# Layer 3's expert feed-forward: an expert's rows turned between the two products of the expert before it, and result rows scattered to their tokens' rows in DRAM

## Chip, cores and metric

The kernel runs on one core of one Trainium2 chip. The metric is the device time of one execution in microseconds (us), given as the median of three runs.

## The reference

The whole model has four layers on 2 images of 256 channels and 48 x 48 pixels, so T = 4608 tokens of C = 256 numbers. The change touches the second half of layer 3 alone, a mixture of eight experts in which each token goes to one expert:

```
x = layer-normalised tokens, [4608, 256]
idx  = argmax(softmax(x @ gate_w + gate_b))      # the token's expert
prb  = that expert's probability
pos  = the token's place among the tokens of its expert, in token order
kept = pos < 720                                 # capacity: ceil(1.25 * 4608 / 8)
buf[idx, pos] = x                                # 8 x 720 slots of 256; others stay zero
hmid = relu(buf @ w1[e] + b1[e])                 # 256 -> 1024
ybuf = hmid @ w2[e] + b2[e]                      # 1024 -> 256
y    = ybuf[idx, min(pos, 719)] * prb * kept     # dropped tokens get zero
t    = t + nan_to_num(y, 0, 1e4, -1e4)
```

With the reference's own inputs (seed 0) the router is very uneven. Counting `idx` in the reference gives 0, 0, 0, 3148, 37, 804, 607 and 12 tokens for experts 0 to 7. With the capacity of 720 that leaves 2096 slots of 5760 with a token, 3664 empty slots (all of experts 0, 1 and 2, nearly all of 4 and 7), and 2512 tokens that are dropped.

## The kernel before

Activations are kept with channels on the partitions: `E.xres` is the residual stream, [128, 2, 4608], in SBUF for the whole kernel. Layers 0 to 2 and layer 3's attention come first. While that attention runs, class `Gate` works behind it: `take` writes the normalised tokens as rows of 256 numbers to DRAM (`xt_d`), and `place` works out for each slot which token it holds. It leaves three small tables in SBUF: `token` (the token of each slot; an empty slot gets token 0), `share_s` (its probability; zero for an empty slot) and `get` (for each token the row of `ybuf` with its result; the zero row behind the last slot for a dropped token). A slot is known by its expert, one of six groups (`JT`) and one of 120 places in the group (`JP`).

`layer3` then has two stages, each in pools of its own, and all instructions stand in program order on in-order engines, but for what the framework's scheduler moves.

**Experts**, for e in 0 to 7. The weights of e + 1 are asked for on SP's queue (L1742 to L1746). GpSimd issues six indirect gathers of 120 rows of 1 KB from `xt_d` into `xe` (L1770). TensorE turns them with twelve 120x120 transposes into `tp` (L1779, two PSUM buffers), VectorE copies four `tp` into `xT` (L1783). The first product `ph` (L1790) has 64 matmul instructions, since an f32 matmul is two; ScalarE writes `hid` with relu (L1794). The second product `py` (L1805) has 96 instructions over six groups. Two groups at a time VectorE adds the bias (L1809), multiplies by the share (L1811), and builds `fin`, the value with NaN and infinities replaced (L1817 to L1823); `fin` has two buffers and is first set to zero by GpSimd (L1815). SP stores `fin` to its slots' rows in `ybuf` (L1825).

**Return**, for 36 blocks of 128 tokens. GpSimd gathers each token's row of `ybuf` by `get` (L1835, six buffers), TensorE turns it with two transposes (L1841), VectorE adds it to `xres` (L1843). `store_out` (L1850) then has SP store `xres` to the output in twelve pieces of 384 KB, each as soon as its three blocks are done.

Of the kernel before, what the change touches and what calls it, by code (L numbers as in the profile page):

```python
# [1451 lines left out]
class Gate:  # L1452
# [8 lines left out]
    def __init__(self, E, keep, wp):  # L1461
        nc, p = E.nc, E.p
        self.JP = JP = self.CAP // self.JT
        self.NJ = NJ = self.NX * self.JT
        NX = self.NX
        self.wp = wp
        self.xt_d = E.dram.tile([T, C], F32, name="xt_d")
        self.get = keep.tile([P, NT], I32, name="get")
        self.token = keep.tile([JP, NJ], I32, name="token")
        self.share_s = keep.tile([JP, NJ], F32, name="share_s")  # L1470

        self.tg = wp.tile([P, 2, P + NX], F32, name="tg")
        nc.sync.dma_start(self.tg[:, :, P:], p["m_gate_w"].rearrange("(k p) e -> p k e", p=P))
        nc.vector.tensor_copy(self.tg[:, :, :P], bc(E.ident, [P, 2, P], 1))
        self.lg = wp.tile([P, NT, NX], F32, name="lg")

        self.gsum = wp.tile([P, NX], F32, name="gsum")
        self.both = wp.tile([P, NX], F32, name="both")
        self.gb = wp.tile([P, NX], F32, name="gb")
        nc.sync.dma_start(self.gb, p["m_gate_b"].partition_broadcast(P))  # L1480
        ids_i = wp.tile([P, P], I32, name="ids_i")
        nc.gpsimd.iota(ids_i, pattern=[[1, P]], base=0, channel_multiplier=0)
        self.ids = wp.tile([P, P], F32, name="ids")
        nc.vector.tensor_copy(self.ids, ids_i)
        part_i = wp.tile([P, 1], I32, name="part_i")
        nc.gpsimd.iota(part_i, pattern=[[0, 1]], base=0, channel_multiplier=1)
        part = wp.tile([P, 1], F32, name="part")
        nc.vector.tensor_copy(part, part_i)
        self.upto = wp.tile([P, P], F32, name="upto")
        nc.vector.tensor_scalar(self.upto, self.ids, part, None, ALU.is_ge)  # L1490
        self.ones = wp.tile([P, P], F32, name="ones")
        nc.vector.memset(self.ones, 1.0)

        tid_i = wp.tile([P, NT], I32, name="tid_i")
        nc.gpsimd.iota(tid_i, pattern=[[P, NT]], base=1, channel_multiplier=1)
        self.tid = wp.tile([P, NT], F32, name="tid")
        nc.vector.tensor_copy(self.tid, tid_i)

        self.before = wp.tile([P, NX], F32, name="before")
        nc.vector.memset(self.before, 0.0)  # L1500
        self.table = wp.tile([JP, 2, NJ], F32, name="table")
# [48 lines left out]
    def place(self, E, a, b, ps):  # L1550
# [90 lines left out]
            nc.vector.tensor_scalar(self.token, self.table[:, 0, :], -1.0, 0.0, ALU.add, ALU.max)  # L1641
            nc.vector.tensor_copy(self.share_s, self.table[:, 1, :])

        nc.vector.scalar_tensor_tensor(pos, idx, float(CAP), pos, ALU.mult, ALU.add)
        nc.vector.tensor_tensor(pos, pos, over, ALU.add)
        nc.vector.tensor_scalar(self.get[:, bs], pos, float(NX * CAP), None, ALU.min)
        yield


# [71 lines left out]
def layer3(ctx, E):  # L1721

    nc, tc, p = E.nc, E.tc, E.p
    NX, FT, CAP, JT = Gate.NX, 8, Gate.CAP, Gate.JT
    JP = CAP // JT
# [1 line left out]
    FMAX = 3.4028234663852886e38  # L1729
    keep = ctx.enter_context(tc.tile_pool(name="l3keep", bufs=1))  # L1730
    wts = ctx.enter_context(tc.tile_pool(name="l3wt", bufs=2))
    ybuf = E.dram.tile([NX * CAP + 1, C], F32, name="ybuf")
    limit = keep.tile([P, 2, C], F32, name="limit")
    nc.vector.memset(limit[:, 0, :], 1e4)
    nc.vector.memset(limit[:, 1, :], -1e4)
    zero = keep.tile([1, C], F32, name="zero")
    nc.vector.memset(zero, 0.0)
    nc.sync.dma_start(ybuf[NX * CAP : NX * CAP + 1, :], zero)

    def weights(e):  # L1740
        w1 = wts.tile([P, 2, FT * P], F32, tag="w1", name="w1")
# [8 lines left out]
    with (  # L1750
# [3 lines left out]
        gate = Gate(E, keep, gp)  # L1754
        layer3_attn(E, gate, psl)
        run(gate.place(E, NT - gate.TG, NT, psl))
    token, share_s, get = gate.token, gate.share_s, gate.get

    with (
        tc.tile_pool(name="l3x", bufs=2) as wp,  # L1760
        tc.tile_pool(name="l3xps", bufs=2, space=PSUM) as ps,
    ):
        for e in range(NX):
            w1, w2, b2 = ready
            if e + 1 < NX:
                ready = weights(e + 1)
            xe = wp.tile([JP, JT, C], F32, tag="xe", name="xe")
            for j in range(JT):
                o = e * JT + j
                nc.gpsimd.indirect_dma_start(  # L1770
                    out=xe[:, j, :], out_offset=None, in_=gate.xt_d[:, :],
                    in_offset=bass.IndirectOffsetOnAxis(ap=token[:, o : o + 1], axis=0),
                )
            xT = wp.tile([P, 2, CAP], F32, tag="xT", name="xT")
            for k in range(2):
                for g in range(2):
                    tp = ps.tile([P, HC], F32, tag="tp", name="tp")
                    for j in range(JT // 2):
                        nc.tensor.transpose(  # L1779
                            tp[:, j * JP : (j + 1) * JP],  # L1780
                            xe[:, g * (JT // 2) + j, k * P : (k + 1) * P], E.ident[:JP, :JP],
                        )
                    nc.vector.tensor_copy(xT[:, k, g * HC : (g + 1) * HC], tp)  # L1783
            hid = wp.tile([P, FT, CAP], F32, tag="hid", name="hid")
            for f in range(FT):
                for g in range(2):
                    gs = slice(g * HC, (g + 1) * HC)
                    ph = ps.tile([P, HC], F32, tag="ph", name="ph")
                    for k in range(2):
                        nc.tensor.matmul(  # L1790
                            ph, lhsT=w1[:, k, f * P : (f + 1) * P], rhs=xT[:, k, gs],
                            start=k == 0, stop=k == 1,
                        )
                    nc.scalar.activation(  # L1794
                        hid[:, f, gs], ph, AF.Relu, bias=E.v("m_b1", e * FT + f, 1)
                    )

            JG = 2
            for j0 in range(0, JT, JG):
# [19 lines left out]
                for s, op in enumerate((ALU.is_gt, ALU.is_lt)):  # L1819
                    inf = wp.tile([JP, JG, C], I32, tag="inf", name="inf")  # L1820
                    nc.vector.tensor_scalar(inf, ye, -FMAX if s else FMAX, None, op)  # L1821
                    for j in range(JG):
                        nc.vector.copy_predicated(fin[:, j, :], inf[:, j, :], limit[:JP, s, :])  # L1823
                o = e * CAP + j0 * JP
                nc.sync.dma_start(  # L1825
                    ybuf[o : o + JG * JP, :].rearrange("(j p) d -> p j d", p=JP), fin
                )

    with (
        tc.tile_pool(name="l3y", bufs=6) as wp,  # L1830
        tc.tile_pool(name="l3yps", bufs=4, space=PSUM) as ps,
    ):
        for i in range(NT):
            yt = wp.tile([P, C], F32, tag="yt", name="yt")
            nc.gpsimd.indirect_dma_start(  # L1835
                out=yt, out_offset=None, in_=ybuf[:, :],
                in_offset=bass.IndirectOffsetOnAxis(ap=get[:, i : i + 1], axis=0),
            )
            yp = ps.tile([P, 2, P], F32, tag="yp", name="yp")
            for k in range(2):  # L1840
                nc.tensor.transpose(yp[:, k, :], yt[:, k * P : (k + 1) * P], E.ident)  # L1841
            xr = E.xres[:, :, i * P : (i + 1) * P]
            nc.vector.tensor_tensor(xr, xr, yp, ALU.add)  # L1843


def store_out(E):
# [98 lines left out]
```

## Time and profile before

| | us |
|---|---|
| median of 3 runs | 5459.55 (5452.36 to 5462.36) |
| profiled execution, own time | 5504.47 |
| profiled execution, span of its trace | 5502.7 |
| layer 3's experts, first gather to last `fin` | 5064.2 to 5439.9 |
| return and output, first `yt` gather to the end | 5443.2 to 5502.7 |

The profile is one execution, some 0.8% longer than the median. "PE" is TensorE, "DVE" VectorE, "ACT" ScalarE, "POOL" GpSimd, "SPq" the sync engine's DMA queue. Times are us from the span's start. In the timeline a row holds start, duration, engine, line, operation, out<-in with shapes, the number of instructions, and in square brackets the idle time ahead of them with what ended it. In the table by windows a row holds the window, its length, the busy time of PE, PE's weight loads, DVE, ACT and POOL with their counts, the granted TensorE clock, the busy share of the 16 DMA engines and the GB/s that they moved.

### The profile page before, as it was taken

How to read it: one execution, taken by the hardware profiler on the slowest of the kernel's cores; microseconds unless marked ns; L12 is line 12 of the kernel's file. 1: busy time of each engine (PE TensorE's matmuls, PEld its weight loads, DVE VectorE, ACT ScalarE, POOL GpSimd, SP SyncE). 2: the span in 40 equal slices, each digit the busy share in tenths (PEclk: the TensorE clock that was granted, in tenths of full speed). 3: DMA queues.
4: the chain of work that ended last, by engine and by line, in shares of the span. 5: the costliest groups of instructions: out<-in, count | busy, mean ns of one | idle time of the engine just before them, and what ended most of it. 6: DMA issues, size and time to landing. Idle time of an engine off the chain costs nothing. (4 is left out here: it accounts for less than half of the span.)

```text
span 5502.7 us, 47222 instructions
## 1 busy us (share of the span) xinstructions
PE 4797.7 (87%) x15246; PEld 2649.9 (48%) x15246; DVE 3499.6 (64%) x5380; ACT 2371.5 (43%) x4935; POOL 2398.4 (44%) x1295
## 2 busy tenths in 40 slices
PE   7888788888877787879999999998799999998996
PEld 3444344444333343435555555565455555554664
DVE  4899988888999888999994234456534401212333
ACT  5767777666767566622222123322023322222220
POOL 3888887888989888830000000048412100001112
PEclk8999999999999899999999899999899999999997
DMA  4444444443444444421100100111111100001323
GB/s 155 166 171 177 165 178 160 160 157 137 173 150 173 150 161 153 151 100 37 41 26 2 39 1 0 37 38 24 14 58 46 46 6 6 9 6 23 83 76 80
DMA packets 173646, 486.56 MB, mean 88 GB/s; under 512 B 31487, under 2 KB 96516, under 8 KB 173124
## 3 DMA queue, kind: packets, MB, share of 16 engines
q1 hardware_dynamic: 165252, 471.82, 24.3%
q0 software_dynamic: 8128, 11.55, 1.6%
q8 instruction: 124, 2.03, 0.1%
q14 instruction: 142, 1.16, 0.1%
HBM read 416.44 MB, written 66.86 MB: 88 GB/s over the span
## 5 line engine op out<-in xcount | busy, mean ns | idle before, releaser
L344 PE MATMUL yp<-hc,ident 128*128 128x384 f32 x3072 | 1199.9, 523 | 293.7 <-DVE hc L390 253.8
L359 POOL TENSOR_TENSOR db<-dtu,bb 128x1536 f32<-128x1536 f32 x384 | 1333.3, 3473 | 45.5 <-issue 16.5
L344 PEld LDWEIGHTS yp<-hc,ident 128*128 128x128 f32 x3072 | 574.7, 198 | 875.3 <-DVE hc L390 451.3
L390 POOL TENSOR_TENSOR hc<-ho,cc 128x384 f32<-128x384 f32 x576 | 582.6, 1020 | 183.6 <-DVE ho L382 81.9
L390 DVE TENSOR_TENSOR hc<-hs,cc 128x384 f32<-128x384 f32 x960 | 501.3, 544 | 38.9 <-PE yp L344 37.7
L376 ACT ACTIVATE hs<-dt,negab 128x384 f32<-128x384 f32 x768 | 435.2, 582 | 92.6 <-DVE ho L385 41.4
L376 ACT ACTIVATE hs<-dt,negaf 128x384 f32<-128x384 f32 x768 | 434.6, 582 | 58.4 <-DVE hc L390 27.7
L385 DVE TENSOR_TENSOR_SCAN hs<-hs,state,db 128x384 f32<-128x384 f32 x400 | 396.6, 1015 | 55.8 <-POOL db L359 30.3
L382 DVE TENSOR_TENSOR_SCAN hs<-hs,state,db 128x384 f32<-128x384 f32 x400 | 397.1, 1014 | 30.0 <-POOL db L359 23.2
L1770 POOL DMA_INDIRECT xe<-xt_d,token x48 | 52.4, 1091 | 726.4 <-issue 715.0
L266 PE MATMUL mm<-xw,w_cv 128*128 128x384 f32 x768 | 288.8, 512 | 64.5 <-ACT xs L270 26.6
L1704 PE MATMUL po<-at,xtok 128*128 128x384 f32 x864 | 329.7, 506 | 7.7 <-ACT at L1702 7.5
L912 POOL PARTITION_ALL_REDUCE most<-most x1 | 0.4, 382 | 738.8 <-DVE most L911 738.8
L1354 PE MATMUL ph<-xn,w 128*128 128x384 f32 x768 | 292.9, 523 | 28.0 <-issue 10.4
L1695 PE MATMUL sp<-qT,xn 128*128 128x384 f32 x864 | 317.2, 486 | 0.0
L1702 ACT ACTIVATE at<-sp 128x384 f32<-128x384 f32 x216 | 104.9, 491 | 472.5 <-PE sp L1695 472.4
L1358 ACT ACTIVATE hid<-ph,vec 128x384 f32<-128x384 f32 x192 | 110.8, 582 | 338.8 <-PE ph L1354 254.5
L627 PE MATMUL pf<-t,wfc 128*128 128x384 f32 x768 | 255.4, 489 | 0.0
L646 PE MATMUL po<-hid,wfc 128*128 128x384 f32 x768 | 253.6, 486 | 0.0
L385 DVE TENSOR_TENSOR_SCAN ho<-hs,state,db 128x384 f32<-128x384 f32 x240 | 241.2, 1005 | 15.3 <-ACT hs L376 15.1
L382 DVE TENSOR_TENSOR_SCAN ho<-hs,state,db 128x384 f32<-128x384 f32 x240 | 240.3, 1001 | 6.3 <-ACT hs L376 6.2
L266 PEld LDWEIGHTS mm<-xw,w_cv 128*128 128x128 f32 x768 | 146.0, 196 | 192.7 <-ACT xs L270 43.2
(434 smaller groups left out, 7962.9 us busy)
## 6 DMA issues: line engine op xcount, KB each, us to landing
bb<-bcd SPq DMA_DIRECT2D x192, 768.0 KB
cc<-bcd SPq DMA_DIRECT2D x192, 768.0 KB
xw<-xi_d SPq DMA_DIRECT2D x24, 774.0 KB
w<-in_m_w SPq DMA_DIRECT2D x16, 1024.0 KB
y_d<-y SPq DMA_DIRECT2D x32, 384.0 KB
ye<-y_d SPq DMA_DIRECT2D x32, 384.0 KB
xi_d<-xz SPq DMA_DIRECT2D x48, 192.0 KB
z_d<-xz SPq DMA_DIRECT2D x48, 192.0 KB
```

Of the source, the lines that this page charges most:

```text
L266: nc.tensor.matmul(px, lhsT=w_cv[b, s][:, d * 4 + k, :], rhs=xw[:, d, o : o + W], start=k == 0, stop=k == 3,)
L344: nc.tensor.matmul(yp[d], lhsT=E.ident, rhs=hc, start=False, stop=summed[d] == NS)
L359: nc.gpsimd.tensor_tensor(db, bc(dtu[:, d, :], [P, GN, W], 1), bb, ALU.mult)
L376: nc.scalar.activation(hs, dt[:, d, :], AF.Exp, scale=nega[s][:, d * NS + n : d * NS + n + 1])
L382: nc.vector.tensor_tensor_scan(to, hs, db[:, j], init, ALU.mult, ALU.add)
L385: nc.vector.tensor_tensor_scan(to[:, ::-1], hs[:, ::-1], db[:, j, ::-1], init, ALU.mult, ALU.add)
L390: (nc.gpsimd if on_pool else nc.vector).tensor_tensor(hc, to, cc[:, j, :], ALU.mult)
L627: nc.tensor.matmul(pf, lhsT=wfc1[:, k, f * P : (f + 1) * P], rhs=t1[:, k, :], start=k == 0, stop=k == 1,)
L646: nc.tensor.matmul(po[m], lhsT=wfc2[:, f, m * P : (m + 1) * P], rhs=hid[:, i, :], start=f == 0, stop=f == 15,)
L1354: nc.tensor.matmul(ph, lhsT=w1[:, e, k, f * P : (f + 1) * P], rhs=xn[:, k, c * W : (c + 1) * W], start=k == 0, stop=k == 1,)
L1695: nc.tensor.matmul(sp, lhsT=xn[:, k, t0 + i * P : t0 + (i + 1) * P], rhs=qT[:, k, c * W : (c + 1) * W], start=k == 0, stop=k == 1,)
L1704: nc.tensor.matmul(po[m], lhsT=xtok[:, i, m * P : (m + 1) * P], rhs=at, start=i == 0, stop=i == MT - 1,)
```

## The change

Five things are edited together.

- `Gate.place` leaves out `get`. In its place it works out `out_row`: for each slot the token's row, and row T (4608) for an empty slot.
- `ybuf` is replaced by `y_tok`, [T + 1, 256] in DRAM, whose first T rows are set to zero by 36 stores of 128 KB on SP's queue. In the built program they stand on SP's queue right after layer 2's last small loads (L1265), with that layer's stores `y_d` and loads `ye` among and behind them.
- The gathers (`fetch`) and transposes (`turn`) become functions. Expert 0 is turned ahead of the loop, the rows of e + 1 are turned after the first product of e, and those of e + 2 are fetched after that. In the built program TensorE has, behind the last `ph` of an expert, six transposes, one `py` matmul, three transposes, one `py` matmul, three transposes, and the remaining `py`.
- Each `fin` is scattered by two indirect DMAs of 120 rows on GpSimd's queue to `y_tok` by `out_row`, where SP stored it to `ybuf` before. In the built program every scatter waits for the landing of the scatter before it, since both write `y_tok`; and the `memset` of a `fin` buffer stands right behind a pair of scatters and waits for the second.
- The return has twelve pieces of 384 tokens: one plain load on SP's queue (four buffers), six transposes, two adds. In the built program all twelve loads stand ahead of the twelve output stores on SP's queue; load n + 4 waits for the transposes of piece n.

```diff
@@ -1465,7 +1465,7 @@
         NX = self.NX
         self.wp = wp
         self.xt_d = E.dram.tile([T, C], F32, name="xt_d")
-        self.get = keep.tile([P, NT], I32, name="get")
+        self.out_row = keep.tile([JP, NJ], I32, name="out_row")
         self.token = keep.tile([JP, NJ], I32, name="token")
         self.share_s = keep.tile([JP, NJ], F32, name="share_s")
@@ -1641,9 +1641,11 @@
             nc.vector.tensor_scalar(self.token, self.table[:, 0, :], -1.0, 0.0, ALU.add, ALU.max)
             nc.vector.tensor_copy(self.share_s, self.table[:, 1, :])
-        nc.vector.scalar_tensor_tensor(pos, idx, float(CAP), pos, ALU.mult, ALU.add)
-        nc.vector.tensor_tensor(pos, pos, over, ALU.add)
-        nc.vector.tensor_scalar(self.get[:, bs], pos, float(NX * CAP), None, ALU.min)
+            none = self.wp.tile([JP, NJ], F32, tag="none", name="none")
+            nc.vector.tensor_scalar(none, self.table[:, 0, :], 0.0, float(T + 1), ALU.is_equal, ALU.mult)
+            nc.vector.scalar_tensor_tensor(
+                self.out_row, self.table[:, 0, :], -1.0, none, ALU.add, ALU.add
+            )
         yield
@@ -1729,13 +1732,14 @@
     FMAX = 3.4028234663852886e38
     keep = ctx.enter_context(tc.tile_pool(name="l3keep", bufs=1))
     wts = ctx.enter_context(tc.tile_pool(name="l3wt", bufs=2))
-    ybuf = E.dram.tile([NX * CAP + 1, C], F32, name="ybuf")
+    y_tok = E.dram.tile([T + 1, C], F32, name="y_tok")
     limit = keep.tile([P, 2, C], F32, name="limit")
     nc.vector.memset(limit[:, 0, :], 1e4)
     nc.vector.memset(limit[:, 1, :], -1e4)
-    zero = keep.tile([1, C], F32, name="zero")
-    nc.vector.memset(zero, 0.0)
-    nc.sync.dma_start(ybuf[NX * CAP : NX * CAP + 1, :], zero)
+    zero = keep.tile([P, C], F32, name="zero")
+    nc.gpsimd.memset(zero, 0.0)
+    for i in range(NT):
+        nc.sync.dma_start(y_tok[i * P : (i + 1) * P, :], zero)
     def weights(e):
         w1 = wts.tile([P, 2, FT * P], F32, tag="w1", name="w1")
@@ -1754,16 +1758,13 @@
         gate = Gate(E, keep, gp)
         layer3_attn(E, gate, psl)
         run(gate.place(E, NT - gate.TG, NT, psl))
-    token, share_s, get = gate.token, gate.share_s, gate.get
+    token, share_s, out_row = gate.token, gate.share_s, gate.out_row
     with (
         tc.tile_pool(name="l3x", bufs=2) as wp,
         tc.tile_pool(name="l3xps", bufs=2, space=PSUM) as ps,
     ):
-        for e in range(NX):
-            w1, w2, b2 = ready
-            if e + 1 < NX:
-                ready = weights(e + 1)
+        def fetch(e):
             xe = wp.tile([JP, JT, C], F32, tag="xe", name="xe")
             for j in range(JT):
                 o = e * JT + j
@@ -1771,9 +1772,12 @@
                     out=xe[:, j, :], out_offset=None, in_=gate.xt_d[:, :],
                     in_offset=bass.IndirectOffsetOnAxis(ap=token[:, o : o + 1], axis=0),
                 )
+            return xe
+        def turn(xe):
             xT = wp.tile([P, 2, CAP], F32, tag="xT", name="xT")
-            for k in range(2):
-                for g in range(2):
+            for g in range(2):
+                for k in range(2):
                     tp = ps.tile([P, HC], F32, tag="tp", name="tp")
                     for j in range(JT // 2):
                         nc.tensor.transpose(
@@ -1781,6 +1785,14 @@
                             xe[:, g * (JT // 2) + j, k * P : (k + 1) * P], E.ident[:JP, :JP],
                         )
                     nc.vector.tensor_copy(xT[:, k, g * HC : (g + 1) * HC], tp)
+            return xT
+        xT = turn(fetch(0))
+        xe = fetch(1)
+        for e in range(NX):
+            w1, w2, b2 = ready
+            if e + 1 < NX:
+                ready = weights(e + 1)
             hid = wp.tile([P, FT, CAP], F32, tag="hid", name="hid")
             for f in range(FT):
                 for g in range(2):
@@ -1794,6 +1806,10 @@
                     nc.scalar.activation(
                         hid[:, f, gs], ph, AF.Relu, bias=E.v("m_b1", e * FT + f, 1)
                     )
+            if e + 1 < NX:
+                xT = turn(xe)
+            if e + 2 < NX:
+                xe = fetch(e + 2)
             JG = 2
             for j0 in range(0, JT, JG):
@@ -1821,26 +1837,31 @@
                     nc.vector.tensor_scalar(inf, ye, -FMAX if s else FMAX, None, op)
                     for j in range(JG):
                         nc.vector.copy_predicated(fin[:, j, :], inf[:, j, :], limit[:JP, s, :])
-                o = e * CAP + j0 * JP
-                nc.sync.dma_start(
-                    ybuf[o : o + JG * JP, :].rearrange("(j p) d -> p j d", p=JP), fin
-                )
-
+                for j in range(JG):
+                    o = e * JT + j0 + j
+                    nc.gpsimd.indirect_dma_start(
+                        out=y_tok[:, :], in_=fin[:, j, :], in_offset=None,
+                        out_offset=bass.IndirectOffsetOnAxis(ap=out_row[:, o : o + 1], axis=0),
+                    )
+    TG = gate.TG
     with (
-        tc.tile_pool(name="l3y", bufs=6) as wp,
-        tc.tile_pool(name="l3yps", bufs=4, space=PSUM) as ps,
+        tc.tile_pool(name="l3y", bufs=4) as wp,
+        tc.tile_pool(name="l3yps", bufs=3, space=PSUM) as ps,
     ):
-        for i in range(NT):
-            yt = wp.tile([P, C], F32, tag="yt", name="yt")
-            nc.gpsimd.indirect_dma_start(
-                out=yt, out_offset=None, in_=ybuf[:, :],
-                in_offset=bass.IndirectOffsetOnAxis(ap=get[:, i : i + 1], axis=0),
+        for c in range(NT // TG):
+            yt = wp.tile([P, TG, C], F32, tag="yt", name="yt")
+            nc.sync.dma_start(
+                yt, y_tok[c * W : (c + 1) * W, :].rearrange("(i p) d -> p i d", p=P)
             )
-            yp = ps.tile([P, 2, P], F32, tag="yp", name="yp")
             for k in range(2):
-                nc.tensor.transpose(yp[:, k, :], yt[:, k * P : (k + 1) * P], E.ident)
-            xr = E.xres[:, :, i * P : (i + 1) * P]
-            nc.vector.tensor_tensor(xr, xr, yp, ALU.add)
+                yp = ps.tile([P, W], F32, tag="yp", name="yp")
+                for i in range(TG):
+                    nc.tensor.transpose(
+                        yp[:, i * P : (i + 1) * P], yt[:, i, k * P : (k + 1) * P], E.ident
+                    )
+                xr = E.xres[:, k, c * W : (c + 1) * W]
+                nc.vector.tensor_tensor(xr, xr, yp, ALU.add)
 def store_out(E):
```

## The prediction

> **What bounds the kernel now.** I read the cores first: one core, 5502.7 us, clock 0.949. The page then has TensorE busy for 87% of the span, but only layer 3's end is touched, from the first `xe` gather at 5064.2 to the end at 5502.7, so I read that stretch by its waits, timeline and windows. The waits between 5097 and 5440 us, seven of the eight experts:
>
> ```profile
> engine line waited for: us in total, times, longest us
> POOL fin L1815 <- DMA ybuf<-fin: 275.9, 17, 31.4
> PE ph L1790 <- DVE xT L1783: 16.1, 7, 2.3
> PE tp L1779 <- DVE xT L1783: 3.0, 7, 0.4
> ```
>
> TensorE sets the pace of the experts, and what stops it is one thing: at each change of expert it waits for `xT`, 16.1 + 3.0 = 19.1 us in 7 changes. GpSimd's long waits hold up nothing. The timeline of the last change and of the end:
>
> ```profile
> 5392.65 1.45 DVE L1823 COPY_PREDICATED fin<-inf,limit 120x256 f32<-120x256 int32 x4
> 5393.99 0.97 DVE L1783 COPY xT<-tp 128x360 f32<-128x360 f32 x2
> ...
> 5394.57 20.36 PE L1790 MATMUL ph<-xT,w 128*128 128x360 f32 x60 [2.30 <-DVE xT L1783]
> ...
> 5414.77 20.88 PE L1805 MATMUL py<-w,hid 128*120 128x256 f32 x96
> ...
> 5424.62 1.45 DVE L1823 COPY_PREDICATED fin<-inf,limit 120x256 f32<-120x256 int32 x4
> ...
> 5431.53 1.44 DVE L1823 COPY_PREDICATED fin<-inf,limit 120x256 f32<-120x256 int32 x4
> ...
> 5438.42 1.45 DVE L1823 COPY_PREDICATED fin<-inf,limit 120x256 f32<-120x256 int32 x4
> 5443.20 0.99 POOL L1835 DMA_INDIRECT yt<-ybuf,get  x1 [14.04 <-DMA ybuf<-fin]
> ...
> 5449.63 49.48 SPq L1850 DMA_DIRECT2D out<-xres  x12
> ```
>
> The two `xT` copies stand on VectorE behind the preceding expert's last `fin`; that is the wait. From the last expert's `py` (call its start S = 5414.77) the three `fin` end at S+11.3, S+18.2 and S+25.1, the return starts at S+28.4, and the end is at S+87.9: 59.5 us for return and output. Windows show what these are limited by:
>
> ```profile
> 5079.00:5093.00 14.00, 12.68 (x42) 7.71 (x41) 0.00 (x0) 5.51 (x10) 6.89 (x7) 1.00 0.87 79
> 5121.00:5123.00 2.00, 0.75 (x4) 0.17 (x2) 2.00 (x6) 0.00 (x0) 1.29 (x1) 1.00 1.00 345
> 5125.00:5131.00 6.00, 6.00 (x21) 3.65 (x20) 0.00 (x0) 3.05 (x6) 3.86 (x5) 1.00 0.45 129
> 5450.00:5475.00 25.00, 10.89 (x35) 4.92 (x35) 6.65 (x16) 0.00 (x0) 16.86 (x19) 0.50 0.80 172
> 5475.00:5499.00 24.00, 9.96 (x32) 4.45 (x31) 6.89 (x17) 0.00 (x0) 12.04 (x13) 0.50 0.81 176
> ```
>
> The last two columns are DMA share and GB/s. Gathers for the empty experts 0 to 2, where all 120 rows are token 0's row, keep the DMA engines 0.87 busy for 79 GB/s (row 1). Those of expert 3, with 720 different tokens, need 0.45 for 129 (row 3). So repeated reads of one 1 KB row cost some three times as much per byte: a 120 KB gather takes about 1.5 us of transfer against 0.4. The return is in the same state: 2512 of its 4608 rows are the one zero row, and it runs at 172 to 176 GB/s with the DMA engines 0.8 busy.
>
> **What the skill says.** The Trainium skill, "DMA: Bandwidth & Descriptors", section "Anatomy of one DMA", gives a fixed cost of about 2.0 us to each DMA, most of it until the write is confirmed; the trace agrees (the 240 KB store of `fin` lands 2.44 us after its start). The same page, "Rules for kernel authors", says of a scatter with a repeated index that each duplicate's write goes out on its own: so the 3664 empty slots all cost a write to row T; no scatter is in this trace. "SBUF — State Buffer", section "A bandwidth-pool intuition that's wrong", gives one HBM port about 22.5 GB/s. The 79 GB/s of row 1 would be three to four such ports (an estimate from that figure); it is for reads. "TensorE: Matmul & The Clock Gate", Part 1: half clock until about 3.4 us of sustained work; the windows of the return show 0.50.
>
> **The change, part by part**, against the profiled 5504.47 us (span 5502.7 and 1.8 around it).
>
> *Turning between the products.* Removed: the 19.1 us. Moved: 12 transposes (0.16 us each) and four copies (0.53) per expert to behind the last `ph`, where VectorE has been idle for some 20 us. The third group of transposes needs the first copy out of `tp`: that is done about 0.47 + 0.1 + 0.53 = 1.1 us in, and TensorE arrives after six transposes and a `py` (two instructions of 0.22) at 0.94 + 0.43 = 1.4. Nothing waits; I allow 0.15 per change, 1.1 in all. Gain 18 (15 to 19). Expert 0's start stays: its sixth gather is issued at 5070.65 and lands at 5075.5 with either order. The gathers of e + 2 move past SP's queue nowhere and past the scatters on POOL's, with an expert's slack. `out_row` is needed 35 us after it is made, so its two instructions, and `get`'s nine (0.17 each), cost nothing.
>
> *Zero stores.* 36 issues of 0.3 to 0.4 us on SP, 4.7 MB, from about 4013 us. Behind them on SP are `y_d` (4028 before) and `ye` (4035 before), first used by GpSimd at 4103.67; 68 us of cover. Cost 0, at most 2.
>
> *Scatters.* Removed: 24 stores on SP. Added: 48 scatters on POOL, in a chain. Let X be the time from one scatter to the next: a gap of 0.30 and a start of 0.98 (the gathers' rows), then the landing. The trace has no scatter; the nearest is the first same-row gather, 5064.18 to its use at 5068.12, 3.94 us, so X = 4.2. Lower bound 3.0 (the 2.44 us store with GpSimd's start in place of SP's); upper bound 5.7, if writes to one row go at half the speed of the reads. A pair is 2X, then the memset 0.6. Per expert POOL has 6X + 1.8 + 7.7 (six gathers at 1.28) = 35 us, inside TensorE's 42. Queued behind a waiting scatter are the memset (VectorE's third `fin` needs it at S+22.7) and the next gathers. For the last expert: pair 1 runs S+11.3 to 19.7, memset to 20.3 (no stall), pair 2 to 28.7, 29.3, pair 3 to 37.7; SP's loads start at S+38.0, where the gathers started at S+28.4. Cost 9.6 (X = 3.0: S+31.4, cost 3; X = 5.7: S+47, cost 18.6).
>
> *Return.* Removed: 36 gathers, one per 1.25 us. Added: 12 plain loads of 393 KB in 1 KB rows. The load of `w2`, also 1 KB rows, ran at 345 GB/s (row 2): 1.1 us each. The lone last store moved 393 KB in the 1.5 us after 5499.5. TensorE has six transposes per piece, 1.85 us at half clock and about 1.0 when warm; since it is busy most of the time it should warm up. The first piece lands at 2.5; the eighth is turned at about 13.5 (warm) to 17.7 (cold), counted from the first load. Only then is load 12 issued, and behind it the stores, the first eight at once: 13.2 us of stores plus 1.5 of remaining loads and 2.3 for the last landing and the end. That is 31 to 35; I take 33 against 59.5: gain 26.5 (19.5 if loads and stores disturb each other and it takes 40; 30.5 at 29).
>
> *Sum.* -18 + 9.6 - 26.5 = -34.9: 5504.5 becomes 5469.6. The runs are shorter by 5459.55/5504.47 = 0.992, so 34.6 there: 5425.
>
> **The rivals.**
>
> *Scatters a bit dearer or cheaper*, X at its ends: 3.0 gives -18 + 3 - 26.5 = -41.5, 5418; 5.7 gives -26, 5434. For the low end: writes may be confirmed without queueing. For the high end: 120 writes to one address.
>
> *The return is limited by DMA anyway*: 9.4 MB at the 174 GB/s of now is 54 us, with 3 around it 57, gain 2.5; sum -11, 5449. For it: the DMA engines are 0.8 busy there. Against: expert 3's gathers and `w2` show that the share comes from the one row, which plain loads don't read repeatedly.
>
> *Slower: row T serialises the scatters.* Above X = 5.4 POOL's 6X + 9.8 exceeds TensorE's 42.1. Experts 0, 1 and 2 have nothing but empty slots, so the lag adds up over three: at X = 8 it is 3 x 15.7 = 47, less the 9 that VectorE can be late before the next `xT` copies are (25 - 2X): TensorE stands 38. The end pays too: loads from S+60.8, cost 32. Sum -18 + 38 + 32 - 26 = +26, 5485. It decides from X of about 7, a landing of 6 us, 27 GB/s for 120 rows of 1 KB. For it: 3664 of 5760 writes hit one row. Against: reads of one row do 79.
>
> *The turning gains nothing*, since VectorE's copies wait for `fin` again: only when a pair is later than S+40, X over 12.
>
> **How the numbers follow.** Main case 0.50 (5415 to 5440, forecast 5425); cheap end 0.18 (5418); dear end 0.14 (5434); DMA-limited return 0.08 (5449); slower 0.09 (5485); turning without gain 0.01. The range to leave out the last three is 5410 to 5446. About 0.2%, 11 us, is what a measurement of this kernel can tell from no change: faster 0.83, same 0.08, slower 0.09.
>
> **What would show it.** Right: no TensorE wait on `xT` at the changes, a period near 42.3 where it was 45.3; scatters about 4 us apart in experts 0 to 2 and nearer 3.4 in 3 and 5; loads starting near 38 us after the last `py`'s start; return and output near 33. Wrong: scatters more than 5.4 apart with `py` or `xT` late behind `fin`, or a DMA share near 1 with under 200 GB/s in the return.

## The result, and the profile after

| | before | after |
|---|---|---|
| median of 4 runs each, us | 5457.56 (5452.36 to 5462.36) | 5414.51 (5406.22 to 5416.97) |
| ratio after / before | | 0.9919, 95% interval 0.9908 to 0.9931 |
| profiled execution, own time (span) | 5504.47 (5502.7) | 5416.49 (5414.7) |

The change takes 43 us off, where 34.6 was forecast (5425).

The two profiles differ by 88 us, not 43. The first gather of `xe` starts at 5064.18 in the profile of before and at 5019.63 in that of after, a difference of 44.6 us that lies upstream of everything the change was costed on. In the eleven other profiles of this study, two of them of kernels built on the kernel before, that gather starts between 5004 and 5028. So the profiled execution of before is one that lost some 45 us in layer 2's work on edges (the sum of line 1236 begins at 4009 us there, and between 3949 and 3970 in every other profile). Most of it stands in one place: VectorE is idle for 44.2 us before the copy of line 957 there, and for 9.4 us in each of the twelve other profiles. What it waited for the profile doesn't show. I therefore compare from the first `xe` gather to the end: 438.5 us before, 395.1 after, 43.4 less, which is what the medians say.

That stretch has three parts. S is again the start of the last expert's `py`, R the start of the return (the first gather, or the issue of the first load):

| | first gather to S | S to R | R to the end | sum |
|---|---|---|---|---|
| before | 350.6 | 28.4 | 59.5 | 438.5 |
| after | 324.0 | 36.9 | 34.1 | 395.1 |
| difference | -26.6 | +8.5 | -25.4 | -43.5 |

**The experts.** In the waits of after between 5095 and 5390 us TensorE's matmuls wait for nothing before the return; what is left of the waits on `xT` is this one of weight loads, in 6 changes together (columns: in total, times, longest):

```profile
engine line waited for: us in total, times, longest us
...
PE yp L1860 <- DMA yt<-y_tok: 20.0, 2, 19.7
...
PEld tp L1783 <- DVE xT L1787: 1.7, 6, 0.3
```

The timeline of TensorE at one change of expert in after:

```profile
5136.48 0.78 PE L1783 MATMUL tp<-ident,xe 120*128 120x120 f32 x6
5137.09 0.60 PE L1821 MATMUL py<-w,hid 128*120 128x256 f32 x2
5137.58 0.53 PE L1783 MATMUL tp<-ident,xe 120*128 120x120 f32 x3
5137.94 0.60 PE L1821 MATMUL py<-w,hid 128*120 128x256 f32 x2
5138.37 0.47 PE L1783 MATMUL tp<-ident,xe 120*128 120x120 f32 x3
5138.68 20.02 PE L1821 MATMUL py<-w,hid 128*120 128x256 f32 x92
5158.54 19.52 PE L1802 MATMUL ph<-xT,w 128*128 128x360 f32 x64
```

No row has a bracket, so TensorE never stops. `ph` follows `py` at once, where the prediction's lines of before had 2.30 us of idle time ahead of it. From one expert's first `py` to the next it is 41.4 us (5095.67, 5137.09, 5178.52), and so it is for all experts but the last, which comes after 40.8 since no transposes stand among the `py` before it.

**The last expert and the return.** The timeline of after, from the first `fin` of the last expert (S = 5343.61):

```profile
5353.47 1.44 DVE L1839 COPY_PREDICATED fin<-inf,limit 120x256 f32<-120x256 int32 x4
...
5354.88 1.00 POOL L1842 DMA_INDIRECT y_tok<-fin,out_row  x1 [19.13 <-DVE fin L1839]
...
5361.28 1.38 POOL L1842 DMA_INDIRECT y_tok<-fin,out_row  x1 [5.40 <-DVE fin L1839]
...
5365.53 1.00 POOL L1842 DMA_INDIRECT y_tok<-fin,out_row  x1 [0.18 <-DVE ye L1827]
...
5369.43 0.99 POOL L1842 DMA_INDIRECT y_tok<-fin,out_row  x1 [2.90 <-DVE fin L1839]
5373.32 1.00 POOL L1842 DMA_INDIRECT y_tok<-fin,out_row  x1 [2.90 <-DMA y_tok<-fin,out_row]
5377.21 0.99 POOL L1842 DMA_INDIRECT y_tok<-fin,out_row  x1 [2.89 <-DMA y_tok<-fin,out_row]
5380.55 16.94 SPq L1854 DMA_DIRECT2D yt<-y_tok  x12
...
5397.55 11.77 SPq L1871 DMA_DIRECT2D out<-xres  x12
```

Six scatters stand in one chain. The bracket of the last two names what they wait for, the landing of the scatter before (the moment at which its end is signalled). A link is the time from one scatter's start to the next one's: the first takes 6.4 us, the second, with a `memset` in it, 4.25, the other three 3.9. The loads start 3.3 us after the last scatter, at S+36.9. The windows of the return in after, in which the last two columns are again DMA share and GB/s:

```profile
5380.50:5384.00 3.50, 0.00 (x0) 0.00 (x0) 0.00 (x0) 0.00 (x0) 0.00 (x0) 0.50 0.71 190
5384.00:5396.00 12.00, 7.94 (x44) 6.57 (x45) 7.19 (x14) 0.00 (x0) 0.00 (x0) 0.78 0.86 273
5396.00:5402.60 6.60, 5.07 (x30) 4.40 (x28) 4.83 (x11) 0.00 (x0) 0.00 (x0) 0.78 0.78 254
5402.60:5414.70 12.10, 0.00 (x0) 0.00 (x0) 0.47 (x2) 0.00 (x0) 0.00 (x0) 0.63 0.85 318
```

At 0.78 to 0.86 busy the DMA engines now move 254 to 273 GB/s, where the gathers of before got 172 to 176.

### The profile page after: what moved, and what is told of

It reads as the page before. It is cut to its first block, busy times and chain, and to the rows that moved or that the text cites. A ratio compares the mean times of both kernels' runs of the same rounds, so it can differ in the third digit from the quotient of the medians.

```text
span 5414.7 us, 47212 instructions
## 1 busy us (share of the span) xinstructions
PE 4771.7 (88%) x15246; PEld 2653.7 (49%) x15246; DVE 3503.3 (65%) x5360; ACT 2365.8 (44%) x4935; POOL 2410.2 (45%) x1308
## 5 line engine op out<-in xcount | busy, mean ns | idle before, releaser
L359 POOL TENSOR_TENSOR db<-dtu,bb 128x1536 f32<-128x1536 f32 x384 | 1332.3, 3471 | 49.7 <-issue 19.1
L376 ACT ACTIVATE hs<-dt,negab 128x384 f32<-128x384 f32 x768 | 434.2, 581 | 93.3 <-DVE ho L385 42.1
L376 ACT ACTIVATE hs<-dt,negaf 128x384 f32<-128x384 f32 x768 | 433.4, 581 | 55.0 <-DVE hc L390 25.5
L385 DVE TENSOR_TENSOR_SCAN hs<-hs,state,db 128x384 f32<-128x384 f32 x400 | 395.1, 1010 | 56.0 <-POOL db L359 30.3
L1354 PE MATMUL ph<-xn,w 128*128 128x384 f32 x768 | 288.2, 519 | 19.3 <-ACT hid L1358 7.6
L392 ACT COPY state<-hs 128x1 f32<-128x1 f32 x800 | 117.5, 155 | 278.2 <-DVE hc L390 276.3
```

What stands on the lines that cost most here:

```text
L359: nc.gpsimd.tensor_tensor(db, bc(dtu[:, d, :], [P, GN, W], 1), bb, ALU.mult)
L376: nc.scalar.activation(hs, dt[:, d, :], AF.Exp, scale=nega[s][:, d * NS + n : d * NS + n + 1])
L385: nc.vector.tensor_tensor_scan(to[:, ::-1], hs[:, ::-1], db[:, j, ::-1], init, ALU.mult, ALU.add)
L1354: nc.tensor.matmul(ph, lhsT=w1[:, e, k, f * P : (f + 1) * P], rhs=xn[:, k, c * W : (c + 1) * W], start=k == 0, stop=k == 1,)
```

## The experiments

What was open: why the experts gained 26.6 and not 18; whether the two halves of the change are independent; what sets the links of the scatters; what limits the return, before and after. The stretches of all profiles, in the columns of the table above, are what most verdicts rest on. Two runs of one kernel differ upstream by 10 us and more, so edits worth 2 to 10 us show here rather than in the time:

| kernel | to S | S to R | R to end | sum |
|---|---|---|---|---|
| e1 turning only | 324.0 | 28.4 | 60.2 | 412.6 |
| e2 rows only | 350.5 | 37.0 | 32.0 | 419.5 |
| e3 spare rows | 323.6 | 34.2 | 32.3 | 390.1 |
| e4 before, many zero rows | 350.6 | 28.3 | 54.4 | 433.4 |
| e5 twelve loads | 323.7 | 36.7 | 30.5 | 390.8 |
| e6 zero stores twice | 324.3 | 37.0 | 32.2 | 393.4 |
| e7 last expert singly | 323.8 | 30.3 | 34.5 | 388.5 |
| e8 four edits | 323.9 | 29.5 | 30.0 | 383.4 |
| e9 no clamp in the last | 323.8 | 32.3 | 31.5 | 387.7 |
| after, again | 323.8 | 37.0 | 32.0 | 392.7 |
| e8, again | 322.4 | 29.5 | 31.1 | 382.9 |

**e1: the turning alone.** The kernel before, with `fetch` and `turn` as in the change and nothing else:

```diff
+        xT = turn(fetch(0))
+        xe = fetch(1)
         for e in range(NX):
...
+            if e + 1 < NX:
+                xT = turn(xe)
+            if e + 2 < NX:
+                xe = fetch(e + 2)
```

> The turning between the products alone: the rows still go to slots and come back by gathers. Theory read from the two traces: the period of an expert goes from 44.85 us (an undisturbed one before) to 41.4 us, as in the changed kernel, so 7 x 3.4 = 24 us less: 5434 beside 5457.6 (ratio 0.9956). Rival A, the prediction's own sum (only the 2.7 us of waits on xT per change go): 18 us less, 5439.5 (0.9967), and the period stays at 42.1 or more. Rival B: the turning pays only together with the scatters: under 5 us less. No TensorE wait on xT in any case but B.

Measured: 5433.31 us, ratio 0.9956 (0.9942 to 0.9969). The interval holds rival A's 0.9967 too, so the trace decides. The periods are 41.4 us, where rival A has 42.1 or more. To S it is 324.0 us, the same as after, and TensorE waits for nothing from the first expert's first `py` to S. The whole of the 26.6 comes from the turning, and it needs nothing of the scatters.

**e2: the scatters and the return alone.** The changed kernel, each expert's rows fetched and turned at its own start again:

```diff
-        xT = turn(fetch(0))
-        xe = fetch(1)
         for e in range(NX):
...
+            for j in range(JT):
+                o = e * JT + j
+                nc.gpsimd.indirect_dma_start(
...
+                        nc.tensor.transpose(
...
+                    nc.vector.tensor_copy(xT[:, k, g * HC : (g + 1) * HC], tp)
...
-            if e + 1 < NX:
-                xT = turn(xe)
-            if e + 2 < NX:
-                xe = fetch(e + 2)
```

> The scatters, the zero stores and the plain return alone: each expert's rows are turned at its own start again, as before. Theory: the period stays near 44.9 us, the loads start 36 to 38 us after the last expert's py (8 to 9 later than the gathers did) and return and output take 34 instead of 59.5, so 17 us less: 5440.5 (ratio 0.9969). Rival: with the scatters on GpSimd the third fin comes later, and VectorE's xT copies behind it, so the change of expert costs more than before (waits on xT over 25 us instead of 19 in 7 changes) and the gain is under 12 us.

Measured: 5439.63 us, ratio 0.9971 (0.9960 to 0.9983); the stretch is 19.0 shorter than before. The waits of TensorE from the first to the last expert in e2:

```profile
engine line waited for: us in total, times, longest us
PE ph L1794 <- DVE xT L1787: 16.3, 7, 2.5
PE tp L1783 <- DVE xT L1787: 3.0, 7, 0.4
```

19.3 us in 7 changes, as before (19.1). The scatters on GpSimd make no `fin` late, and the rival falls. The halves add: 0.9956 x 0.9971 = 0.9927, and the stretches -25.9 and -19.0 make -44.9, against -43.4 together.

**Where the experts' other 8.6 us come from** can be read from e1, e2 and before, with no further run. The seven periods of before are not alike: five take 44.8 us and two 46.4; in e2 and e4 it is four and three. In after and e1 all take 41.4, but for the last with 40.8. TensorE's timeline of before at an ordinary change and at one of the two long ones:

```profile
5168.84 1.48 PE L1790 MATMUL ph<-xT,w 128*128 128x360 f32 x4 [2.32 <-DVE xT L1783]
5170.15 0.27 PE L1779 MATMUL tp<-ident,xe 120*128 120x120 f32 x1
5170.43 17.21 PE L1790 MATMUL ph<-xT,w 128*128 128x360 f32 x56
...
5213.67 1.48 PE L1790 MATMUL ph<-xT,w 128*128 128x360 f32 x4 [2.30 <-DVE xT L1783]
5214.99 0.36 PE L1779 MATMUL tp<-ident,xe 120*128 120x120 f32 x1
5215.26 18.77 PE L1790 MATMUL ph<-xT,w 128*128 128x360 f32 x56
```

The waits are equal, yet the same 56 matmuls take 18.77 us instead of 17.21. The windows of before around the second say why (third column from the right: granted clock):

```profile
5211.00:5213.00 2.00, 0.38 (x2) 0.00 (x0) 2.00 (x6) 0.00 (x0) 1.64 (x2) 1.00 1.06 368
5213.00:5215.00 2.00, 1.33 (x5) 0.81 (x5) 1.06 (x3) 0.36 (x1) 1.68 (x2) 1.00 0.78 197
5215.00:5217.00 2.00, 2.00 (x5) 1.17 (x4) 0.00 (x0) 0.75 (x2) 1.40 (x2) 0.51 0.56 181
5217.00:5219.00 2.00, 2.00 (x5) 1.07 (x4) 0.00 (x0) 0.56 (x1) 1.70 (x3) 0.64 0.38 115
```

After the wait TensorE was granted half its clock: the last two windows lack 1.7 us of full clock, which is 3.4 us at half. It costs 1.55 us. The Trainium skill, "TensorE: Matmul & The Clock Gate", Part 1, gives an idle window of about 3.4 us as what drops the clock; here 2.3 us of wait, 0.44 us of another a little ahead of it, was enough in two of seven changes and in three of seven in e2 and e4, and not enough in the others; what tells them apart stays open. In the kernels without the wait the granted clock is 1.00 from the first expert's first `py` to S. So the sum per change is 2.76 of waits, and 0.66 by which the same matmuls take less: 42.09 us of an ordinary period before, 41.43 after. Taken from each start to the next and without the waits, the twelve transposes take 1.62 us before and 1.29 after, the 64 `ph`, some of which stood beside the waits, 19.75 and 19.36, the 96 `py` 20.72 and 20.78. Together 44.85 - 41.43 = 3.42. Seven of these are 23.9, two dips of the clock 3.1, the last expert's missing transposes 0.6; the first expert's first `py`, with six transposes now ahead of it, is 0.9 later. The sum is 26.7.

**e3: a row of its own for every empty slot.**

```diff
+        nc.gpsimd.iota(self.out_row, pattern=[[JP, NJ]], base=T + 1, channel_multiplier=1)
...
-            nc.vector.tensor_scalar(none, self.table[:, 0, :], 0.0, float(T + 1), ALU.is_equal, ALU.mult)
+            nc.vector.scalar_tensor_tensor(
+                none, self.table[:, 0, :], 0.0, self.out_row, ALU.is_equal, ALU.mult
+            )
...
-    y_tok = E.dram.tile([T + 1, C], F32, name="y_tok")
+    y_tok = E.dram.tile([T + NX * CAP, C], F32, name="y_tok")
```

> The changed kernel, with every empty slot scattered to a spare row of its own (row T + its slot) instead of all of them to row T; the output is the same. Theory (writes to one row queue): the scatters of experts 0, 1, 2, 4 and 7 come to 3.4 to 3.5 us apart, as those of experts 3 and 5 are now, where they were 3.9; in the last expert that is five spacings of 0.45, so the loads start about 2.3 us earlier (S+34.6 instead of S+36.9) and the time is about 2 us lower: 5412, ratio to the changed kernel 0.9996, too little for the time to show. Rival (the row has nothing to do with it; VectorE or the position sets the spacing): they stay 3.9 apart, and the loads start at S+36.9.

Measured: 5408.44 us, ratio to before 0.9918 (0.9903 to 0.9933), not to be told from after. The end of the last expert's chain in e3's timeline:

```profile
5356.60 1.08 POOL L1845 DMA_INDIRECT y_tok<-fin,out_row  x1 [5.02 <-DVE fin L1842]
...
5360.09 1.00 POOL L1845 DMA_INDIRECT y_tok<-fin,out_row  x1 [0.18 <-issue]
5363.53 1.20 POOL L1845 DMA_INDIRECT y_tok<-fin,out_row  x1 [2.44 <-DVE inf L1840]
5367.18 0.99 POOL L1845 DMA_INDIRECT y_tok<-fin,out_row  x1 [2.45 <-DMA y_tok<-fin,out_row]
5370.61 0.99 POOL L1845 DMA_INDIRECT y_tok<-fin,out_row  x1 [2.44 <-DMA y_tok<-fin,out_row]
```

The wait for a landing is 2.45 us instead of 2.90, links behind the first are 3.4 to 3.65 instead of 3.9, and the loads start at S+34.2, near the 34.6 expected. From start to landing most scatters of this chain take 2.6 us, and 3.1 in after. In experts 0 to 2 the undelayed links also came down, from 3.9 to between 3.4 and 3.5. Writes of 120 rows to one row thus cost 0.45 us more than writes to 120 rows. The first link of the last chain stays at 6.0: that is not the row's doing.

Most of the long links of the other experts have a likely cause that neither the prediction nor the expectations named. Expert 3, all of whose slots hold tokens, in after:

```profile
5201.03 0.99 POOL L1842 DMA_INDIRECT y_tok<-fin,out_row  x1 [2.47 <-DVE ye L1827]
...
5207.48 1.00 POOL L1842 DMA_INDIRECT y_tok<-fin,out_row  x1 [0.24 <-issue]
```

This fourth scatter lands only 5.6 us after its start. At 5200.17 SP had asked for 1 MB of weights (L1748), which land 5.8 us later. In expert 6, behind whose products no weights are asked for, the fourth scatter lands after 2.6 us. No run moves these loads, so that they are the cause is not shown.

**e4: the gathers' return, with many zero rows.** The kernel before, but a dropped token reads one of 4608 zero rows:

```diff
-        nc.vector.tensor_scalar(self.get[:, bs], pos, float(NX * CAP), None, ALU.min)
+        nc.vector.tensor_tensor(self.get[:, bs], pos, self.far[:, bs], ALU.min)
...
-    ybuf = E.dram.tile([NX * CAP + 1, C], F32, name="ybuf")
+    ybuf = E.dram.tile([NX * CAP + T, C], F32, name="ybuf")
...
+    for i in range(NT):
+        nc.sync.dma_start(ybuf[NX * CAP + i * P : NX * CAP + (i + 1) * P, :], zero)
```

(`far` is NX * CAP plus the token's number.)

> The kernel before, its return by gathers as it is, but each dropped token reads a zero row of its own region (4608 spare zero rows, written by 36 stores ahead) instead of all 2512 reading one. Theory (GpSimd's 36 gathers at 1.25 us each set the pace of the return, the one row only keeps the DMA engines busy): DMA share in the return falls from 0.8 to about 0.5, the few longer gaps between gathers go, and the time falls by 2 to 4 us at most: 5455 (ratio 0.9994). Rival (the one row limits the return, as the prediction's reading of the DMA share had it): besides the fall of the share, the output stores stop competing with the slow reads and the end comes 8 us or more sooner: 5449 or less (0.9984).

Measured: 5451.70 us, ratio 0.9997 (0.9989 to 1.0006). The profile's return is 5 us shorter, the time cannot be told from before. The windows of e4's return:

```profile
5395.00:5420.00 25.00, 12.89 (x40) 5.90 (x40) 8.21 (x21) 0.00 (x0) 18.91 (x21) 0.50 0.68 212
5420.00:5440.00 20.00, 7.89 (x24) 3.47 (x24) 5.33 (x13) 0.00 (x0) 9.42 (x10) 0.50 0.55 174
```

The DMA engines have less to do (0.68 for 212 GB/s, where it was 0.80 for 172), and still the 36 gathers come every 1.25 us: 0.95 us of GpSimd and 0.30 between two. That pace makes 45 of the return's 54 us. So GpSimd's issue, 36 times 1.25 us, sets the pace of this return. The one zero row is worth some 5 us of it, in the second half: in before and in e1, whose return is the same, the last 15 gathers come every 1.5 us on average, and in e1 they land 7 to 9 us after their start, where those of e4 land after 2.7 to 4.2.

**e5: twelve buffers for the loads.**

```diff
-        tc.tile_pool(name="l3y", bufs=4) as wp,
+        tc.tile_pool(name="l3y", bufs=12) as wp,
```

> The changed kernel with twelve yt buffers instead of four, so that no load of the return waits for the transposes of an earlier piece. Theory (what held the return at 34.1 us are the loads, 1.7 us apart where w2 ran at 345 GB/s, because only four are in flight): DMA share goes to about 1.0 and 345 to 355 GB/s from 3.3 us after the first load on, the stores begin before R+16 (R is the first load's issue), and return and output take 30.5 to 32 us: 2 to 3.5 us less than the changed kernel, 5411.5 (ratio 0.9995, too little for the time to show; read from the trace). Rival (DMA is the limit as it stands, and the gaps in the profile of the changed kernel were chance; two kernels with the same return took 32.0 and 32.3): return and output 32 or more, no gain beyond those.

Measured: 5409.73 us, ratio to before 0.9905 (0.9885 to 0.9925). The return is 30.5 us. The windows of e5's return:

```profile
5387.60:5398.00 10.40, 8.88 (x51) 7.71 (x52) 8.24 (x16) 0.00 (x0) 0.00 (x0) 0.74 1.10 353
5398.00:5408.00 10.00, 3.04 (x23) 2.17 (x21) 4.12 (x9) 0.00 (x0) 0.00 (x0) 0.93 1.06 389
```

With all loads asked for at once the DMA engines are full from 3.3 us on, at 353 to 389 GB/s. 9.4 MB at these rates take 24 to 27 us, so a return of 30.5 that moves them has little left to gain. But part of the gap to after was chance: seven profiles with four buffers have returns of 31.5 to 34.5 us (mean 32.7), three with twelve have 30.0 to 31.1. Twelve buffers are worth about 2 us, not 3.6.

**e6: the zero stores twice.**

```diff
-    for i in range(NT):
+    for i in 2 * list(range(NT)):
```

> The changed kernel with the zero stores issued twice (72 instead of 36, 9.4 MB). Theory (they are hidden in 68 us of cover before the first use of what is queued behind them on SP): no change, 5414.5 within 2 us; from the acc of L1236 to the first gather of xe still 1057.8 us. Rival (they cost something that the comparison of two profiles left unseen, such as the 2.6 us by which this stretch is longer in the changed kernel than before): 2.6 us or more on that stretch, and in the time (ratio to before 0.9924 instead of 0.9919).

Measured: 5414.73 us, ratio 0.9913 (0.9895 to 0.9930). From the sum of line 1236 to the first gather of `xe` it is 1057.9 us (after: 1057.8). In all profiles this stretch lies between 1052.6 and 1061.5, with 0, 36 or 72 zero stores; the 2.6 us by which after was longer than before are within that. Two profiles without zero stores have a mean of 1058.0, ten with 36 have 1057.4; a cost of 1 or 2 us could hide in this.

**e7: the last expert's groups singly.**

```diff
-            JG = 2
+            JG = 2 if e + 1 < NX else 1
```

> The changed kernel, but in the last expert (alone) VectorE finishes and GpSimd scatters the rows one group of 120 at a time instead of two. Theory (the tail between the last py and the return is the chain of six scatters, not TensorE or VectorE): the first scatter starts about 4 us sooner, at S+7.5, the chain then runs 3.9 us a link with a memset here and there, and the loads start at S+31 to S+34 instead of S+36.9: 3 to 6 us less, 5410 (ratio to before 0.9911). Rival (VectorE, which now does twice as many small operations, or its use of the SBUF beside GpSimd, stretches the links to 5 us and more): the loads start at S+36 or later and nothing is gained.

Measured: 5404.50 us, ratio to before 0.9902 (0.9885 to 0.9918). The first scatter starts at S+6.8, the loads at S+30.3, 6.7 sooner than in after. The chain of scatters, not TensorE or VectorE, is what stands between the last `py` and the return.

**e9: without the clamp in the last expert.** The question is the first link of 6.4 us. Left out is the replacing of infinities, in the last expert alone:

```diff
-                for s, op in enumerate((ALU.is_gt, ALU.is_lt)):
+                for s, op in enumerate((ALU.is_gt, ALU.is_lt) if e + 1 < NX else ()):
```

> The changed kernel without the clamp of infinities (L1835 to L1839: two comparisons and four predicated copies for each fin, 2.3 us of VectorE) in the last expert; that part of the computation is left out. In the changed kernel the first link of the last expert's chain takes 6.4 us (S+11.3 to S+17.7) where the others take 3.9, though the data is ready and the first scatter's data has moved by S+13.6. Theory (VectorE, busy without a gap from S+14.0 to S+18.2, keeps GpSimd from starting): with VectorE's work shortened the first scatter starts at S+9, all links are near 3.9, and the loads start at S+31.5 to S+33 instead of S+36.9, 4 to 5.5 us less. Rival (the first link of the last chain is long for another reason): it stays at 6 us or more, and the loads start at S+34.5 or later.

Measured: 5407.76 us, ratio to before 0.9916 (0.9902 to 0.9929). The last chain in e9's timeline (S = 5342.16):

```profile
5351.93 1.00 POOL L1842 DMA_INDIRECT y_tok<-fin,out_row  x1 [17.65 <-DVE fin L1834]
5356.70 0.99 POOL L1842 DMA_INDIRECT y_tok<-fin,out_row  x1 [3.78 <-issue]
...
5360.57 1.00 POOL L1842 DMA_INDIRECT y_tok<-fin,out_row  x1 [0.18 <-DVE ye L1827]
5363.94 0.99 POOL L1842 DMA_INDIRECT y_tok<-fin,out_row  x1 [2.37 <-DMA y_tok<-fin,out_row]
```

The first link falls from 6.4 to 4.8 us and the loads start at S+32.3, so VectorE's work has a part in that delay. By itself it does not make it. The same operations, as close together, stand beside the first link of expert 6 in after:

```profile
5314.81 1.00 POOL L1842 DMA_INDIRECT y_tok<-fin,out_row  x1 [17.89 <-DVE fin L1839]
5318.25 0.99 POOL L1842 DMA_INDIRECT y_tok<-fin,out_row  x1 [2.44 <-DVE ye L1825]
```

That link takes 3.44 us, and those of experts 0, 1 and 3 to 5 take 3.5 to 4.0. In all of these the second scatter starts 0.8 us after the first has landed, in the last expert 3.4 us after. Whether the moment of the landing among VectorE's operations decides, which differs by some tenths of a us, or something that the last expert alone has, stays open.

Two links of e9's chain are 3.4 us although all their rows go to row T. The landings take 3.1 us there as everywhere in this chain, so the 0.45 us of e3 are paid; it is the next scatter that starts 0.3 us after a landing instead of 0.8.

**e8: four edits together**, e3, e5, e7 and this one, which keeps the `memset` out of the chain:

```diff
-                fin = wp.tile([JP, JG, C], F32, tag="fin", name="fin")
+                fin = wp.tile([JP, 2, C], F32, tag="fin", name="fin", bufs=6)[:, :JG]
```

> The changed kernel with four edits together: a spare row for every empty slot, the last expert's groups one at a time, six fin buffers (so that no memset stands between two scatters of the last expert), twelve yt buffers. Theory (each takes its link out of the tail; links 3.45 us): loads at S+28 to S+30, return and output 30.5 to 32, together 9 to 12 us less than the changed kernel: 5404 (ratio to before 0.9900). Rival (the tail is held by VectorE's last fin or by the DMA alone, so the gains don't add): under 5 us less, 5410 or more.

Measured: 5404.57 us, ratio to before 0.9899 (0.9879 to 0.9918). The last chain and the return in e8's timeline (S = 5346.90):

```profile
5353.71 1.00 POOL L1845 DMA_INDIRECT y_tok<-fin,out_row  x1 [15.30 <-DVE fin L1842]
5359.75 0.99 POOL L1845 DMA_INDIRECT y_tok<-fin,out_row  x1 [5.04 <-DVE inf L1840]
5363.19 0.99 POOL L1845 DMA_INDIRECT y_tok<-fin,out_row  x1 [2.45 <-DVE inf L1840]
...
5370.07 1.00 POOL L1845 DMA_INDIRECT y_tok<-fin,out_row  x1 [2.45 <-DVE inf L1840]
5373.51 0.99 POOL L1845 DMA_INDIRECT y_tok<-fin,out_row  x1 [2.44 <-DMA y_tok<-fin,out_row]
```

All links but the first are 3.44 us; the first is 6.04, the loads start at S+29.5. To settle what it is worth, it was timed with the changed kernel on one chip:

> The changed kernel as it is, for the comparison with the next one on one chip: 5414 within 5 us; return and output 32 to 34 us, loads at S+36.9.

> The kernel with the four edits together, beside the changed kernel on one chip. By the stretch from the first gather of xe to the end it is 11.7 us shorter in the profiles (383.4 instead of 395.1), so 5414 becomes 5402.5. Rival (something upstream pays part of it back, as equal medians of this kernel and the one with the last expert's groups alone could mean): under 6 us less.

Measured: after 5401.40 us (ratio to before 0.9915, 0.9901 to 0.9928), e8 5397.45 (0.9908, 0.9893 to 0.9924). Both are lower than expected; in their profiles the first gather of `xe` starts at 5004 and 5011 us, 16 and 12 sooner than in the first profiles of the same kernels. By the stretch, e8 is 10.7 us shorter than after (means of two profiles each, 383.1 and 393.9). By the time it is 4 us here and, by the first ratios (0.9899 and 0.9919), 11; the intervals overlap. The stretch is shown to be shorter; that the whole kernel is, is likely but not shown.

## Why the prediction was right, and where its sizes were off

**Direction and range: right.** 5414.5 lies in 5410 to 5446. The sum had three terms, and each of them appears in the trace with its sign.

**The turning, forecast -18 (15 to 19), measured -26.6.** This is the term that failed in size, outside its own bounds, and all of the 8.6 us between forecast and result. The mechanism was right: the waits on `xT` are gone and nothing took their place. The step "Removed: the 19.1 us" counted the wait alone. Not counted were the clock that a wait sometimes takes along (3.1) and the matmuls, transposes and `ph`, that take less with no wait among them (0.66 per change, 4.6 in seven); and the allowance of 1.1 for stalls was not needed. The first and the last expert take 0.3 of this away again. The clock was legible: the prediction used a mean period of 45.3 over periods of which five were 44.8 and two 46.4. That the matmuls would take less no trace of before showed.

**Zero stores, forecast 0, at most 2:** no cost is seen, with twice as many either (e6), to within the 9 us by which the stretch varies.

**The scatters, forecast +9.6 with X = 4.2, measured +8.5.** X is 3.9 for one row and 3.45 for 120 rows (forecast 3.4). That the sum came out near is partly luck, since errors offset. From the first scatter to the loads 26.7 us were forecast and 25.7 measured. The first link took 6.4, 2.2 more than X; the four others were 0.3 shorter each; of the two `memset`s in the forecast's chain only one stands there, and costs 0.35 where 1.2 were put down; and the loads start 3.3 us after the last scatter, not X + 0.3 = 4.5. The first link was on no list. The Trainium skill, "SBUF — State Buffer", section "SBUF: two separate sides", warns of one way to such a delay: while VectorE runs an operation in a mode that takes the port it shares with GpSimd, GpSimd cannot write a DMA's descriptors. That e9 shortens the link agrees; that the same operations leave the first link of six other experts at 3.4 to 4.0 says that they do not bring it about by themselves, and which operation would hold the port the runs don't show.

**The return, forecast 33 us, measured 34.1, and 32.7 as a mean of seven profiles: right in size.** The reasons are half right. The loads were to come every 1.1 us, and with four buffers came every 1.4 (16.9 us for twelve). And the reading that the return of before was in the state of the same-row gathers, so that the one zero row limits it, holds for some 5 us only (e4): GpSimd's 1.25 us per gather was the pace. The prediction had that number and wrote the removed gathers down as such, so the sum did not suffer.

**Scaling.** The forecast multiplied the profile's time by 0.992. The excess of that profile lay in layer 2, so the local difference stood in the median as it was; it made 0.3 us here.

**The rivals.** DMA-limited return (5449): out, 30 to 34 us instead of 57. A cheap or a dear scatter (X of 3.0 or 5.7): out, with 3.9. Row T serialising (5485): the links of experts 0 to 2, all empty slots, average 4.3 to 4.4 with their delays, and TensorE never waited. There is room left: in experts 0 to 2 the last scatter of an expert starts some 34 us after its first `py`, and TensorE's period is 41. Turning without gain: out by e1.

## What to carry to other kernels

A short wait of TensorE costs its own length and sometimes the clock after it. Moving the next unit's transposes between two products of this one removed both here, and needed no other change. When many small indirect DMAs are replaced, count what each takes on GpSimd's queue (1.25 us here) before blaming the DMA engines' share. Where scatters write one tensor, the built program here made them a chain of landings. What mattered of it was only the part behind the last product, and starting the chain sooner shortened that.

## What was not expected of the hardware

- A wait of 2.3 us was followed by 3.4 us at half of TensorE's clock in 2 of 7 changes in one profile and in 3 of 7 in two others, at a cost of 1.55 us each; in the ten profiles without the wait the clock stayed at 1.00.
- An indirect scatter of 120 rows of 1 KB takes 0.99 us of GpSimd and, with nothing beside it, lands 2.6 us after its start when its rows differ and 3.1 when they are one row. The difference of 0.45 us stands against 1.1 us that the prediction worked out for reads of one row, from their 79 GB/s.
- A scatter with 1 MB of weights on the way beside it landed after 5.6 us instead of 2.6 (expert 3 in after).
- The first link of the last chain took 6.4 us instead of 3.9, and 4.8 with part of VectorE's operations left out; the same operations stood beside the first links of six other experts, which took 3.4 to 4.0.
